# Scan tiles of two states by 64 channels, with the product by C on GpSimd

## The chip, the cores and the metric

The kernel runs on one core of one Trainium2 chip. A core has five engines that run their own instruction queues in order: TensorE (PE), VectorE (DVE), ScalarE (ACT), GpSimd (POOL) and SyncE (SP, which here only issues DMAs). The metric is the device time of one execution in microseconds; lower is better.

## The reference

The input x has the shape (8, 512, 48, 48): 8 samples, 512 channels, 2304 tokens. Two layers follow each other, each behind a group norm and with a residual sum. The first is causal linear attention with 8 heads. The second cuts the 512 channels into four blocks of 128 and runs a Mamba block on each in turn; each block's input is its own 128 channels plus the result of the block before. The part that the change touches is the recurrence inside a Mamba block, over 256 inner channels d and 16 states n:

```
delta = softplus(dt @ Wdt.T + bdt)                 # (tokens, 256)
dA  = exp(delta[d] * A[d, n]);  dBu = delta[d] * xs[d] * B[n]
h   = dA_t * h + dBu_t                             # for every token t
y_t = sum over n of h[d, n] * C_t[n]   + xs * D
out = (y * silu(z)) @ Wo.T
```

A[d, n] comes from a stored logarithm, B and C come from a projection of xs and differ for each token, not for each channel. All data are fp32.

## The kernel before

The 2304 tokens are cut into 6 chunks of `LC` = 384. For each sample, each of its four blocks (called scales in the code) and each chunk there are two functions.

`prepare` makes a chunk's inputs. PE multiplies the tokens with the convolution's taps (`xc`) and ACT makes `xs` (Silu); PE makes `z` and ACT the gate `sz`; PE makes the rows B, C and dt (`dbc`), ACT copies them out (`dbcs`), and SP writes B and C to scratch memory (`scr`). PE makes `v`, and the softplus of it is put together from Abs, Exp and Ln on ACT, one step on DVE (L332), two on POOL (L333, L334) and one on DVE (L335). DVE multiplies `dx` = delta * xs (L337). `prepare` of chunk c+1 stands in the program ahead of the scan of chunk c.

`scan` runs the recurrence. The partitions hold 128 channels, so there are two halves h; states are taken two at a time (`NG` = 2). For each pair, SP loads `bc` (L348): B and C of both states, 384 tokens each, sent to all 128 partitions, 768 KB; the pool holds two such tiles, and both halves use one. For each half ACT makes `dA` = exp(delta * A) for each state (L353), DVE makes `u` = B * dx for both (L357, 768 columns), DVE runs one `tensor_tensor_scan` for each state (L360, 384 columns), POOL copies the last column into `state` for the next chunk (L369), DVE multiplies by C (L370, 768 columns), and PE adds the products up over the states, as a matmul with the identity into the PSUM tile `yp` (L372). A last matmul with a diagonal matrix adds xs * D (L376). That makes 32 scans for a chunk. Then DVE multiplies `yp` by the gate (`yz`, L412), PE projects (`xm`, L415) and DVE takes the maximum (`fg`, L418). After the sixth chunk two means over all tokens give two sigmoids, and the next block starts from the result; nothing of the next block can start before.

The attention of the next sample is cut into 18 chunks of 128 tokens, which are spread over the last two blocks of the current sample. The attention of the first sample runs alone at the start. Its steps go through PE (`qk` L157, `v` L176, `kc` L186 and more), ACT (`ex` L168, `rl` L169) and DVE by turns; POOL makes its input `xn` (L148).

A scheduler orders the instructions of each engine's queue when the program is built, and puts in the waits. A queue runs in that order, so an instruction that waits holds everything behind it.

Of the kernel before, what the change touches and what calls it, by code (L numbers as in the profile page):

```python
# [9 lines left out]
F32 = mybir.dt.float32  # L10
# [7 lines left out]
T = 128  # tokens of an attention chunk  # L18
LC = 384  # tokens of a chunk of the state-space scan
NG = 2  # states that share one broadcast load and one product instruction  # L20
C_ID, C_MASK, C_GRP, C_ALL, C_TRI, C_SEL, C_BC = 0, 128, 256, 384, 512, 640, 672
C_END = C_BC + 512


def constants():
    """Matrices that the shapes alone give."""
    c = np.zeros((P, C_END), np.float32)
    p = np.arange(P)
    c[:, C_ID : C_ID + P] = p[:, None] == p[None, :]
    c[:, C_MASK : C_MASK + P] = p[:, None] <= p[None, :]  # L30
    c[:, C_GRP : C_GRP + P] = np.where(p[:, None] // 16 == p[None, :] // 16, 1.0 / 16.0, 0.0)
    same = p[:, None] % 64 == p[None, :] % 64
    c[:, C_ALL : C_ALL + P] = same
    c[:, C_TRI : C_TRI + P] = same & (p[:, None] // 64 <= p[None, :] // 64)
    for t in range(4):
        for half in range(2):
            head = 2 * t + half
            c[half * 64 : half * 64 + 64, C_SEL + t * 8 + head] = 1.0
            c[head, C_BC + t * P + half * 64 : C_BC + t * P + half * 64 + 64] = 1.0
    return c  # L40
# [3 lines left out]
def attention_then_mamba_kernel(  # L44
    ctx: ExitStack,
    tc: tile.TileContext,
    x: bass.AP,  # (B, 512, L)
    consts: bass.AP,
    wqkv: bass.AP,  # (512, 1536): input channel, output channel
    bqk: bass.AP,  # (128, 8)  # L50
    bv: bass.AP,  # (1, 512)
    win: bass.AP,  # (4, 128, 512): input channel, output channel
    wconv: bass.AP,  # (4, 1, 1024): tap, channel
    bconv: bass.AP,  # (4, 128, 2)
    wxp: bass.AP,  # (4, 128, 2, 40): columns B, C, dt
    wdt: bass.AP,  # (4, 8, 256)
    bdt: bass.AP,  # (4, 1, 256)
    alog: bass.AP,  # (4, 128, 2, 16)
    dskip: bass.AP,  # (4, 128, 2)
    wout: bass.AP,  # (4, 128, 2, 128)  # L60
    out: bass.AP,  # (B, 512, L)
# [15 lines left out]
    ps1 = ctx.enter_context(tc.tile_pool(name="ps1", bufs=4, space=PSUM))  # L77
    ps2 = ctx.enter_context(tc.tile_pool(name="ps2", bufs=1, space=PSUM))
# [10 lines left out]
    hbc = cst[0:8, C_BC : C_BC + 512].rearrange("p (t m) -> p t m", t=4)  # L89

# [13 lines left out]
    def group_norm(xt, name):  # L104
        """Scale and offset per channel, (128, 2), that normalise each 16 channels of xt."""
# [23 lines left out]
    def attention(b, X):  # L129
        """Puts x + attention(group norm of x) into X, a tile for each 128 channels; pauses  # L130
        after each chunk of tokens."""
# [11 lines left out]
        for i in range(L // T):  # L143
# [7 lines left out]
            # elu(t) + 1 = max(t, 0) + min(exp(t), 1)  # L151
# [30 lines left out]
            # The denominator: q . (sum of k over this head and those before it)  # L182
# [23 lines left out]
            # The numerator is linear in q, so q carries the denominator.  # L206
# [3 lines left out]
            for par in range(2):  # L210
                rows = slice(par * 64, par * 64 + 64)
                sc = one_bank(f"sc{par}_{n}").rearrange("p (o t) -> p o t", o=4)
                for o in range(4):
                    nc.tensor.matmul(sc[:, o, :], kT[rows, o, :], qT[rows, o, :], start=True, stop=True)
                m = apool.tile([P, 4, T], F32, tag=f"sm{par}", name=f"sm{par}_{n}")
                nc.vector.tensor_mul(m, sc, mask.unsqueeze(1).to_broadcast([P, 4, T]))
                sm.append(m)
# [15 lines left out]
            if i + 1 < L // T:  # L233
# [3 lines left out]
                kl = apool.tile([P, 4, P], F32, tag="kl", name=f"kl_{n}")  # L237
# [11 lines left out]
    def load_scale(b, s):  # L249
        """The weights of one of the four blocks."""  # L250
# [3 lines left out]
        # The convolution's taps scale the columns of the projection in front of it.  # L254
# [16 lines left out]
        dd = wpool.tile([P, 2, P], F32, tag="dd", name=f"dd_{n}")  # L271
        for h in range(2):
            nc.gpsimd.tensor_scalar_mul(dd[:, h, :], ident, pv[:, 2 + h : 3 + h])
        av = wpool.tile([P, 2, NS], F32, tag="av", name=f"av_{n}")
# [5 lines left out]
    def prepare(n, c, w, xi):  # L280
        """Projections of a chunk: its inputs to the scan, and the gate."""
        wi, wk, wo, wx, wd, pv, dd, av = w
        c0 = c * LC
        xc = ps2.tile([P, 2, 512], F32, tag="pp", name=f"xc_{n}_{c}")
        xs = mpool.tile([P, 2, LC], F32, tag="xs", name=f"xs_{n}_{c}")
        for h in range(2):
            for k in range(4):
                nc.tensor.matmul(  # L288
                    xc[:, h, 0:LC],
# [4 lines left out]
                )  # L294
        for h in range(2):
            nc.scalar.activation(xs[:, h, :], xc[:, h, 0:LC], AF.Silu, bias=pv[:, h : h + 1])
        zp = ps2.tile([P, 2, 512], F32, tag="pp", name=f"z_{n}_{c}")
        for h in range(2):
            nc.tensor.matmul(
                zp[:, h, 0:LC],  # L300
# [5 lines left out]
        sz = mpool.tile([P, 2, LC], F32, tag="sz", name=f"sz_{n}_{c}")  # L306
        nc.scalar.activation(sz, zp[:, :, 0:LC], AF.Silu)

        # B, C, dt, and a row of ones for dt's bias
# [9 lines left out]
        # softplus(v) = max(v, 0) + log1p(y), y = exp(-|v|);  # L319
        # log1p(y) = log(1 + y) + (y - ((1 + y) - 1)), the second term for the sum's rounding  # L320
        vp = ps2.tile([P, 2, 512], F32, tag="pp", name=f"v_{n}_{c}")
        for h in range(2):
            nc.tensor.matmul(
                vp[:, h, 0:LC], wd[32:41, h * P : (h + 1) * P], dbc[32:41, :], start=True, stop=True
            )
        y = mpool.tile([P, 2, LC], F32, tag="y", name=f"y_{n}_{c}", bufs=1)
        nc.scalar.activation(y, vp[:, :, 0:LC], AF.Abs)
        nc.scalar.activation(y, y, AF.Exp, scale=-1.0)
        delta = mpool.tile([P, 2, LC], F32, tag="delta", name=f"delta_{n}_{c}")
        nc.scalar.activation(delta, y, AF.Ln, bias=1.0)  # L330
# [3 lines left out]
        nc.gpsimd.tensor_tensor(delta, delta, y1, ALU.add)  # L334
        nc.vector.scalar_tensor_tensor(delta, vp[:, :, 0:LC], 0.0, delta, ALU.max, ALU.add)  # L335
        dx = mpool.tile([P, 2, LC], F32, tag="dx", name=f"dx_{n}_{c}", bufs=1)
        nc.vector.tensor_mul(dx, delta, xs)  # L337
        return xs, sz, scr, delta, dx

    def scan(n, c, w, pre, state):  # L340
        """The recurrence over a chunk, all states: D x + sum of C h."""
        wi, wk, wo, wx, wd, pv, dd, av = w
        xs, sz, scr, delta, dx = pre
        yp = psy.tile([P, 2, 512], F32, tag="yp", name=f"yp_{n}_{c}")
        src = scr.rearrange("(m n) l -> m n l", m=2)
        for g in range(0, NS, NG):
            bc = mpool.tile([P, 2, NG, LC], F32, tag="bc", name=f"bc_{n}_{c}_{g}")
            nc.sync.dma_start(out=bc, in_=src[:, g : g + NG, :].partition_broadcast(P))  # L348
            for h in range(2):
                m = f"{n}_{c}_{g}_{h}"  # L350
                dA = mpool.tile([P, NG, LC], F32, tag="dA", name=f"dA_{m}", bufs=3)
                for j in range(NG):
                    nc.scalar.activation(  # L353
                        dA[:, j, :], delta[:, h, :], AF.Exp, scale=av[:, h, g + j : g + j + 1]
                    )
                u = mpool.tile([P, NG, LC], F32, tag="u", name=f"u_{m}", bufs=3)
                nc.vector.tensor_mul(u, bc[:, 0], dx[:, h, :].unsqueeze(1).to_broadcast([P, NG, LC]))  # L357
                hs = mpool.tile([P, NG, LC], F32, tag="hs", name=f"hs_{m}")
                for j in range(NG):
                    nc.vector.tensor_tensor_scan(  # L360
                        hs[:, j, :],
                        dA[:, j, :],
                        u[:, j, :],
                        state[:, h, g + j : g + j + 1] if c else 0.0,
# [3 lines left out]
                if c + 1 < NC:  # L368
                    nc.gpsimd.tensor_copy(state[:, h, g : g + NG], hs[:, :, LC - 1])  # L369
                nc.vector.tensor_mul(u, hs, bc[:, 1])  # L370
                for j in range(NG):
                    nc.tensor.matmul(  # L372
                        yp[:, h, 0:LC], ident, u[:, j, :], start=(g + j == 0), stop=False
                    )
        for h in range(2):
            nc.tensor.matmul(yp[:, h, 0:LC], dd[:, h, :], xs[:, h, :], start=False, stop=True)  # L376
        return yp

    def mamba(b, X):
        """The four blocks in turn, from X to the output; pauses after each chunk of tokens."""  # L380
# [4 lines left out]
        for s in range(4):  # L385
# [4 lines left out]
            state = small.tile([P, 2, NS], F32, tag="state", name=f"state_{n}")  # L390
# [16 lines left out]
            for c in range(NC):  # L407
                cols, icols = slice(c * LC, (c + 1) * LC), slice(3 + c * LC, 3 + (c + 1) * LC)
                cur, pre = pre, (prepare(n, c + 1, w, xi) if c + 1 < NC else None)
                yp = scan(n, c, w, cur, state)  # L410
                yz = mpool.tile([P, 2, LC], F32, tag="tmp", name=f"yz_{n}_{c}", bufs=1)
                nc.vector.tensor_mul(yz, yp[:, :, 0:LC], cur[1])  # L412
# [16 lines left out]
            # sigmoids of the two means  # L429
# [15 lines left out]
    # The attention of a sample goes beside the last two blocks of the sample before it, which  # L445
    # leave the tensor engine free, and when two of that sample's four tiles are through.
# [74 lines left out]
```

## Time and profile before

| | |
|---|---|
| median of three runs | 16262.73 us (16234.96 to 16269.74) |
| span of the profiled execution | 16257.6 us |
| DVE busy | 13707.9 us (84%) |
| PE busy | 11687.1 us (72%) |
| ACT busy | 6667.4 us (41%) |
| POOL busy | 4851.7 us (30%) |
| chain that ended last | DVE 51%, PE 27%, issue 15% |

The profiled execution's own time is known as its span, from the first instruction to the last; the median of the runs is 5.1 us above it. The busy share is an average over stages: the attention alone at the start, the first two blocks of each sample (and all four of the last), where DVE has the scan and little else, and the last two blocks of the other samples, where attention shares the engines.

### The profile page before, as it was taken

To read this page: it belongs to the slowest core of one execution; us is meant where nothing else is said; L and a number is where in the kernel's file an instruction comes from. 1 tells how busy PE (TensorE), PEld (TensorE's weight loads), DVE (VectorE), ACT (ScalarE), POOL (GpSimd) and SP (SyncE) were. 2 spreads that over 40 slices of the span, in tenths; PEclk is the share of its full clock that TensorE was granted. 3 is DMA by queue.
4 is the path that set the end of the run, shared out by engine and by line. 5 is a ranking of instruction groups with operands and counts; after the bars stand their busy time and mean duration, and the time that the engine had idled before them with its cause. 6 is when DMAs were issued, how large, how long until landed. Compare 5 with 4: busy or idle time off the path is not lost.

```text
span 16257.6 us, 128122 instructions
## 1 busy us (share of the span) xinstructions
PE 11687.1 (72%) x42400; PEld 6603.9 (41%) x42400; DVE 13707.9 (84%) x16928; ACT 6667.4 (41%) x11513; POOL 4851.7 (30%) x4213
## 2 busy tenths in 40 slices
PE   8766876678766778667786677766777668776666
PEld 6533543235432355334452244533444234442322
DVE  2698888987899878998789987899777998789999
ACT  1344344443444434444334444344443444334444
POOL 0233232332333322332223322233322333223333
PEclk7788998889888889888998889988888888888888
DMA  0133222322233222332223322233222332223333
GB/s 31 49 98 89 72 75 85 99 86 71 77 89 98 85 71 74 92 97 82 71 73 96 98 77 74 69 100 100 76 72 72 100 95 78 66 73 95 96 96 93
DMA packets 470729, 1336.78 MB, mean 82 GB/s; under 512 B 49168, under 2 KB 59696, under 8 KB 461872
## 3 DMA queue, kind: packets, MB, share of 16 engines
q1 hardware_dynamic: 470064, 1328.60, 27.9%
q8 instruction: 334, 5.47, 0.1%
q14 instruction: 331, 2.71, 0.1%
HBM read 1281.28 MB, written 47.19 MB: 82 GB/s over the span
## 4 chain that ended last, share of the span: by engine, by line
DVE 51%; PE 27%; issue 15%; POOL 3%; ACT 3%; DMA 1%; DVEq 0%; SPq 0%; POOLq 0%; ACTq 0%
DVE hs L360 28%; DVE u L357 13%; PE qk L157 6%; DVE u L370 5%; PE yp L372 4%; PE v L176 3%; PE kc L186 2%; PE xm L415 2%; PE o L223 2%; PE xc L288 2%; PE o L220 1%; DVE dx L337 1%; POOL y L333 1%; POOL delta L334 1%; PE ds L241 1%
## 5 line engine op out<-in xcount | busy, mean ns | idle before, releaser
L372 PE MATMUL yp<-u,cst 128*128 128x384 f32 x12288 | 5693.4, 600 | 3126.1 <-DVE u L370 3123.6
L353 ACT ACTIVATE dA<-delta,av 128x384 f32<-128x384 f32 x6144 | 3453.9, 607 | 6896.7 <-DVE hs L360 6827.9
L360 DVE TENSOR_TENSOR_SCAN hs<-dA,state,u 128x384 f32<-128x384 f32 x5120 | 5204.2, 1053 | 25.8 <-ACT dA L353 1.0
L369 POOL COPY state<-hs 128x2 f32<-128x2 f32 x2560 | 3181.9, 1243 | 6692.4 <-DVE hs L360 6692.4
L372 PEld LDWEIGHTS yp<-u,cst 128*128 128x128 f32 x12288 | 2536.7, 225 | 5963.9 <-DVE u L370 4479.3
L357 DVE TENSOR_TENSOR u<-bc,dx 128x768 f32<-128x768 f32 x3072 | 2906.8, 961 | 69.8 <-PE yp L372 65.9
L370 DVE TENSOR_TENSOR u<-hs,bc 128x768 f32<-128x768 f32 x3072 | 2928.6, 953 | 22.6
L288 PE MATMUL xc<-xi,wk 128*128 128x384 f32 x3072 | 1385.8, 592 | 730.4 <-DVE delta L335 597.8
L288 PEld LDWEIGHTS xc<-xi,wk 128*128 128x128 f32 x3072 | 708.7, 237 | 1321.0 <-issue 635.1
L157 PEld LDWEIGHTS qk<-xn,wq_sb 128*128 128x128 f32 x9216 | 1075.8, 196 | 28.3 <-issue 14.0
L157 PE MATMUL qk<-xn,wq_sb 128*128 128x128 f32 x9216 | 1076.6, 279 | 0.0
L360 DVE TENSOR_TENSOR_SCAN hs<-dA,u 128x384 f32<-128x384 f32 x1024 | 974.3, 989 | 8.4
L171 DVE SCALAR_TENSOR_TENSOR f<-ex,rl 128x512 f32<-128x512 f32 x288 | 205.0, 712 | 761.2 <-ACT rl L169 761.2
L148 POOL TENSOR_SCALAR xn<-x,norm_a 128x128 f32<-128x128 f32 x576 | 271.1, 484 | 1719.1 <-PE v L176 1708.2
L353 ACT ACT_TABLE_LOAD x512 | 656.9, 1283 | 8.8
L415 PE MATMUL xm<-yz,wo 128*128 128x384 f32 x768 | 370.6, 615 | 351.9 <-DVE yz L412 351.9
L168 ACT ACTIVATE ex<-qk,bqk_sb 128x128 f32<-128x128 f32 x1152 | 435.8, 378 | 438.3 <-PE qk L157 398.7
L176 PE MATMUL v<-wq_sb,xn 128*128 128x512 f32 x1152 | 518.2, 592 | 0.0
L333 POOL TENSOR_TENSOR y<-y,y 128x768 f32<-128x768 f32 x192 | 416.6, 2170 | 234.2 <-DVE y L332 232.8
L169 ACT ACTIVATE rl<-qk,bqk_sb 128x128 f32<-128x128 f32 x1152 | 441.4, 383 | 0.0
L334 POOL TENSOR_TENSOR delta<-delta,y 128x768 f32<-128x768 f32 x192 | 417.5, 2174 | 15.1
L335 DVE SCALAR_TENSOR_TENSOR delta<-v,delta 128x768 f32<-128x768 f32 x192 | 182.4, 950 | 269.5 <-POOL delta L334 269.5
(98 smaller groups left out, 10133.1 us busy)
## 6 DMA issues: line engine op xcount, KB each, us to landing
bc<-scr SPq DMA_DIRECT2D x1536, 768.0 KB
x<-in_x SPq DMA_DIRECT2D x32, 1152.0 KB
out<-x SPq DMA_DIRECT2D x32, 1152.0 KB
wk<-in_wconv SPq DMA_DIRECT2D x32, 512.0 KB
scr<-dbcs SPq DMA_DIRECT2D x192, 48.0 KB
wi<-in_win SPq DMA_DIRECT2D x32, 256.0 KB
wo<-in_wout SPq DMA_DIRECT2D x32, 128.0 KB
wq_sb<-in_wqkv SPq DMA_DIRECT2D x4, 768.0 KB
```

What stands on the lines that cost most here:

```text
L157: nc.tensor.matmul(ps[:, o, :], wq_sb[:, kt, j * 512 + o * P : j * 512 + (o + 1) * P], xn[:, kt, :], start=(kt == 0), stop=(kt == 3),)
L176: nc.tensor.matmul(vps, xn[:, kt, :], wq_sb[:, kt, 1024:1536], start=(kt == 0), stop=(kt == 3))
L288: nc.tensor.matmul(xc[:, h, 0:LC], wk[:, k, h * P : (h + 1) * P], xi[:, c0 + k : c0 + k + LC], start=(k == 0), stop=(k == 3),)
L333: nc.gpsimd.tensor_tensor(y1, y, y1, ALU.subtract)
L334: nc.gpsimd.tensor_tensor(delta, delta, y1, ALU.add)
L353: nc.scalar.activation(dA[:, j, :], delta[:, h, :], AF.Exp, scale=av[:, h, g + j : g + j + 1])
L357: nc.vector.tensor_mul(u, bc[:, 0], dx[:, h, :].unsqueeze(1).to_broadcast([P, NG, LC]))
L360: nc.vector.tensor_tensor_scan(hs[:, j, :], dA[:, j, :], u[:, j, :], state[:, h, g + j : g + j + 1] if c else 0.0, ALU.mult, ALU.add,)
L369: nc.gpsimd.tensor_copy(state[:, h, g : g + NG], hs[:, :, LC - 1])
L370: nc.vector.tensor_mul(u, hs, bc[:, 1])
L372: nc.tensor.matmul(yp[:, h, 0:LC], ident, u[:, j, :], start=(g + j == 0), stop=False)
L415: nc.tensor.matmul(xm[:, 0:LC], wo[:, h, :], yz[:, h, :], start=(h == 0), stop=(h == 1))
```

## The change

The tile of the scan gets another layout. Its 128 partitions hold two states by 64 channels instead of one state by 128 channels. A half h of 128 channels is then two groups g of 64, and 16 states are 8 pairs. `NG` = 2 now counts pairs, so one group of work holds four scans of 384 columns: two pairs by two channel groups. There are 32 scans for a chunk, as before. Core of the diff:

```diff
-    ps1 = ctx.enter_context(tc.tile_pool(name="ps1", bufs=4, space=PSUM))
-    ps2 = ctx.enter_context(tc.tile_pool(name="ps2", bufs=1, space=PSUM))
+    ps1 = ctx.enter_context(tc.tile_pool(name="ps1", bufs=3, space=PSUM))
+    psa = ctx.enter_context(tc.tile_pool(name="psa", bufs=2, space=PSUM))
+    psx = ctx.enter_context(tc.tile_pool(name="psx", bufs=1, space=PSUM))
     psy = ctx.enter_context(tc.tile_pool(name="psy", bufs=1, space=PSUM))
...
-                m = apool.tile([P, 4, T], F32, tag=f"sm{par}", name=f"sm{par}_{n}")
+                m = apool.tile([P, 4, T], F32, tag=("rl", "ex")[par], name=f"sm{par}_{n}")
...
-                kl = apool.tile([P, 4, P], F32, tag="kl", name=f"kl_{n}")
+                kl = apool.tile([P, 4, P], F32, tag="xn", name=f"kl_{n}")
...
+            nc.scalar.activation(y[:, h, :], vp[:, 0:LC], AF.Abs)
+            nc.scalar.activation(r[:, h, :], vp[:, 0:LC], AF.Relu)
         nc.scalar.activation(y, y, AF.Exp, scale=-1.0)
...
         nc.vector.tensor_scalar(y1, y, 1.0, -1.0, ALU.add, ALU.add)
         nc.gpsimd.tensor_tensor(y1, y, y1, ALU.subtract)
-        nc.gpsimd.tensor_tensor(delta, delta, y1, ALU.add)
-        nc.vector.scalar_tensor_tensor(delta, vp[:, :, 0:LC], 0.0, delta, ALU.max, ALU.add)
-        nc.vector.tensor_mul(dx, delta, xs)
+        nc.gpsimd.tensor_tensor(r, r, y1, ALU.add)
+        nc.scalar.activation(y, y, AF.Ln, bias=1.0)
+        delta = y
+        nc.gpsimd.tensor_tensor(delta, delta, r, ALU.add)
+        dscr = dpool.tile([256, LC], F32, tag="dscr", name=f"dscr_{n}_{c}")
+        nc.sync.dma_start(out=dscr.rearrange("(h p) l -> p h l", h=2), in_=delta)
+        nc.gpsimd.tensor_tensor(dx, delta, xs, ALU.mult)
...
+    def scan(n, c, h, w, pre, state):
+        dr = mpool.tile([P, 2, LC], F32, tag="dr", name=f"dr_{n}_{c}_{h}")
+        dsrc = dscr.rearrange("(h g d) l -> h d g l", h=2, g=2)[h]
+        for i in range(2):
+            nc.sync.dma_start(out=dr[i * 64 : i * 64 + 64], in_=dsrc)
+        dxp = psx.tile([P, 2, 512], F32, tag="dxp", name=f"dxp_{n}_{c}_{h}")
+        for g in range(2):
+            nc.tensor.matmul(dxp[:, g, 0:LC], rep[:, g, :], dx[:, h, :], start=True, stop=True)
+        yp = psy.tile([P, 512], F32, tag="yp", name=f"yp_{n}_{c}_{h}")
+        nc.tensor.matmul(yp[:, 0:LC], dd[:, h, :], xs[:, h, :], start=True, stop=False)
+        for q in range(0, NS // 2, NG):
+            bc = mpool.tile([P, 2, NG, LC], F32, tag="bc", name=f"bc_{m}")
+            for i in range(2):
+                nc.sync.dma_start(out=bc[i * 64 : i * 64 + 64]..., in_=src[q // NG, i].partition_broadcast(64))
+            u = mpool.tile([P, NG, 2, LC], F32, tag="u", name=f"u_{m}", bufs=4)
+            nc.vector.tensor_mul(u, bc[:, 0]..., dxp[:, :, 0:LC]...)
+            for j in range(NG):
+                for g in range(2):
+                    dA = psa.tile([P, 512], F32, tag="dA", name=f"dA_{m}_{j}_{g}")
+                    nc.scalar.activation(dA[:, 0:LC], dr[:, g, :], AF.Exp, scale=...)
+                    nc.vector.tensor_tensor_scan(u[:, j, g, :], dA[:, 0:LC], u[:, j, g, :], ...)
+            if c + 1 < NC:
+                nc.scalar.copy(state[:, h, q : q + NG, :], u[:, :, :, LC - 1])
+            nc.gpsimd.tensor_tensor(u, u, bc[:, 1].unsqueeze(2).to_broadcast(shape), ALU.mult)
+            for j in range(NG):
+                for g in range(2):
+                    nc.tensor.matmul(yp[g * 64 : g * 64 + 64, 0:LC], pair_sum, u[:, j, g, :], start=False, ...)
...
+                for h in range(2):
+                    yp = scan(n, c, h, w, cur, state)
+                    nc.vector.tensor_mul(yz[:, h, :], yp[:, 0:LC], cur[1][:, h, :])
```

In words: delta is written to scratch memory (`dscr`) and read back in the new layout (`dr`); `dx` is copied into it by two matmuls with a 0/1 matrix into PSUM (`dxp`). `dA` goes to PSUM, one bank for each 384 columns, two banks in turn. The scan writes over `u`. A `bc` tile now serves one group of one half, and its two DMAs fetch four rows of 384 in one piece for each of 64 partitions. The state copy moves from POOL to ACT, the product by C from DVE to POOL, and the sum over states becomes a matmul with a 128 by 64 matrix (`pair_sum`) that also adds the two states of a pair. The softplus gets a Relu on ACT, and its last sum and `dx` move from DVE to POOL. `xc`, `z` and `v` now take single banks from the pool `ps1`, which has three banks instead of four and is shared with attention; two attention tiles take over the buffers of others (`sm` those of `rl` and `ex`, `kl` that of `xn`). The host reorders the columns of the projection weights and of A to match.

## The prediction

> **What bounds the kernel now.** I read the totals first, then the chain that ended last, then two stretches, then single rows.
>
> ```profile
> PE 11687.1 (72%) x42400; PEld 6603.9 (41%) x42400; DVE 13707.9 (84%) x16928; ACT 6667.4 (41%) x11513; POOL 4851.7 (30%) x4213
> ...
> DVE 51%; PE 27%; issue 15%; POOL 3%; ACT 3%; DMA 1%; DVEq 0%; SPq 0%; POOLq 0%; ACTq 0%
> ```
>
> DVE leads, but 84% is a mean over stages. The windows view, a plain stretch (scan alone) and one beside attention; columns PE, PEld, DVE, ACT, POOL busy, clock, DMA:
>
> ```profile
> 2700.00:2900.00 200.00, 127.87 (x300) 61.00 (x300) 197.23 (x212) 92.06 (x138) 83.00 (x64) 0.84 0.33 100
> 1800.00:2000.00 200.00, 159.00 (x739) 99.60 (x738) 166.77 (x212) 69.77 (x147) 48.18 (x46) 0.89 0.26 73
> ```
>
> Plain: DVE is busy 197 of 200 us and is the limit. Beside attention it is busy 167, PE 159: engines wait on each other in turn. By the starts of `yz` in the timeline a plain chunk takes 65 us (58 for the sixth, which prepares nothing), the step into the next block 38 more, so a plain block 5 x 65 + 58 + 38 = 421. A sample takes 1993 us, its two blocks beside attention (1993 - 842)/2 = 575.5 each, so each of their nine attention chunks adds 154.5/9 = 17.2. Attention alone ends at 597. Sum: 597 + 18 x 421 + 14 x 575.5 = 16232; 25.6 of the span 16257.6 are the tail, and the median is 5.1 above the span.
>
> The groups of the page (count | busy, mean ns of one | idle before, releaser):
>
> ```profile
> L372 PE MATMUL yp<-u,cst 128*128 128x384 f32 x12288 | 5693.4, 600 | 3126.1 <-DVE u L370 3123.6
> L353 ACT ACTIVATE dA<-delta,av 128x384 f32<-128x384 f32 x6144 | 3453.9, 607 | 6896.7 <-DVE hs L360 6827.9
> L360 DVE TENSOR_TENSOR_SCAN hs<-dA,state,u 128x384 f32<-128x384 f32 x5120 | 5204.2, 1053 | 25.8 <-ACT dA L353 1.0
> L369 POOL COPY state<-hs 128x2 f32<-128x2 f32 x2560 | 3181.9, 1243 | 6692.4 <-DVE hs L360 6692.4
> L357 DVE TENSOR_TENSOR u<-bc,dx 128x768 f32<-128x768 f32 x3072 | 2906.8, 961 | 69.8 <-PE yp L372 65.9
> L370 DVE TENSOR_TENSOR u<-hs,bc 128x768 f32<-128x768 f32 x3072 | 2928.6, 953 | 22.6
> ```
>
> DVE hardly ever waits for ACT (25.8 us): six `dA` of 384 columns are buffered. The others wait for DVE.
>
> **Removed from DVE.** L370 (2928.6), L335 (182.4) and L337 (181.6) go. `u` becomes 1536 instructions of 1536 columns; 768 columns with one operand in PSUM take 0.934 (`yz`, median), 512 take 0.676 (L216, mean), so 1.0 ns a column and 1.73 each: 2657 instead of 2907. Splitting `yz` costs 34. The scan with `dA` in PSUM has no row; `yz` and L357 (medians 0.934 and 0.935) show no price for PSUM, so I keep the busy time, 6178/6144 = 1.01 (ends 0.9 and 1.1). DVE loses 3.5 ms. Its work in a plain chunk is 32 x 1.01 + 8 x 1.73 + 2.4 (`yz`, L332, `fg`) = 48.5 us. If DVE stayed the limit, that would be the gain.
>
> **Added: the product on POOL.** From the views of single lines (min/median/max):
>
> ```profile
> L333 POOL TENSOR_TENSOR y<-y,y x192: 1795/2326/2532, 615.6 to 16129.5; 128x768 f32<-128x768 f32 x192
> ...
> L441 POOL TENSOR_TENSOR x<-x,fg x192: 982/1304/1443, 1015.4 to 16251.5; 128x384 f32<-128x384 f32 x192
> ```
>
> A line through the minima gives 0.98 + 3 x 0.813 = 3.42 us for 1536 columns, through the medians 1.30 + 3 x 1.02 = 4.37. In the timeline L333 takes 1.81 while DVE is idle (at 1038.9) and 2.38 while DVE scans (at 834.3). The new DVE instructions read only one tensor from SBUF and, as shown below, wait often, so I take 3.42 and keep 4.37 as the upper end. With four 768-column steps of 1.8 POOL has 8 x 3.42 + 7.2 + 0.4 = 35 us of work a chunk: no limit by amount.
>
> The Trainium skill, page "SBUF — State Buffer", section on who interferes with whom, says that a DVE instruction with two SBUF inputs contends with a GpSimd instruction that reads SBUF, and one with a single SBUF input does not. By that 3.42 holds and the sum below stands; without it 4.37 does, the third case below.
>
> **Added: a longer turn of `bc`.** This is what the DVE total hides. The two `bc` buffers now serve one group each, and a buffer is free only when POOL's product is done. Before, a `bc` DMA ended 4.8 us after its issue (median, from its packets: first packet at 1.0, then 256 of 3 KB), and the other tile covered 7.9 us. Now it has 128 packets of 6 KB; the 9 KB packets of `out` move 1180 KB in 3.0 us, so 786 KB take 2.0, plus 1.0 and the second issue (0.36, L348): 3.4 to 5.2, I take 3.6. One turn: DMA 3.6, issue 0.1, `u` 1.73, four scans 4.1, state copy on ACT 0.25 (an ACT instruction of 128x32 took 0.23) plus 0.1, product 3.42, other waits 0.3: 13.6 us for two groups, 54.4 a chunk. That is 6.8 a group against DVE's 5.8, so DVE idles 1.0 a group. Bytes for `dr` and `dscr` are 17% more, at a DMA share of 0.33: hidden. On SP, `dscr` waits for POOL's delta ahead of a `bc` whose product comes later on POOL anyway, and `scr` stands between the two halves of a `bc` that is not yet due: nothing. The state copies (8 x 0.25 a chunk) stand on ACT ahead of the next group's second `dA`, under `u`; uncovered they would cost 2 a chunk.
>
> **Added: waits across queues.** `dA` has two banks instead of six tiles, so whatever ACT waits for, DVE waits for two scans later. In the order in which the built program queues its instructions, repeated in the plain blocks, I find in chunks 2, 3 and 4 (a PE pass is 5693.4/12288 = 0.46; two passes a matmul):
> - PE has `v` of the next chunk behind three sums of group 0, which wait for POOL. ACT's Abs waits for `v`, and the third `dA` of the next group stands behind Abs, Relu and Exp. From the last scan: copy 0.35, product 3.42, six passes 2.8, `v` 0.9, four ACT steps of about 0.5, Exp 0.84, `dA` 0.61: 10.9. Cover is `u`, two scans and the idle 1.0, together 4.8. Lost 6.1.
> - `xc` stands behind the four sums of group 0 of the second half, and `xs`, a table load (1.28) and a `dA` behind it: 0.35 + 3.42 + 3.7 + 0.9 + 0.58 + 1.28 + 0.61 = 10.8, lost 6.0. In chunk 1 only half of `xc` is late: 3.
> - `yz` stands in DVE's queue after two scans of the next half and waits for the last product and its four sums: 7.5 against 4.8, plus its own 0.56: 3.3, twice a chunk.
> - Ln waits for POOL's L333 (in place), POOL's next sum for Ln, the next product behind both: 3.
>
> So chunks 2 to 4 take 54.4 + 6.1 + 6.0 + 6.5 + 3.0 = 76.0; chunk 1 66.9; chunk 0, where none of the first two waits stand, 63.9; chunk 5 60.9. Together 419.7. The step into the next block grows from 38 to 48: a third POOL sum instead of L335 (+0.9), `dscr` out and `dr` in, about 2.5 us each (5), product and split steps at the end (+4). A plain block takes 468 instead of 421.
>
> **Attention.** `kl` in the buffer of `xn` makes POOL's four L148 (0.48 each, with a start 2.4) wait for the chunk's last matmuls; alone at the start nothing covers that: 17 x 2.4 = 41, so 638. Beside the scan an attention chunk added 17.2. It could add only its DVE time, 7.6 (1098 us of its DVE rows by 144), filling DVE's waits; or its PE time, 24.1 (3469/144), laid into the chains above. I keep 17.2: 622.5 a block.
>
> **Sum.** 638 + 18 x 468 + 14 x 622.5 + 25.6 + 5.1 = 17808.
>
> PE's added passes (four `dxp` matmuls, 8 x 0.46 a chunk) are inside the waits. The same skill's "TensorEngine Tiling (Array Packing)", section on column tiling, says that matmuls onto 64 columns may run two at a time. L223, which has this form, took 335.0/2304 = 0.145 a pass against 0.121 for L186, so the trace shows no such gain; by the page the sums would halve and the total would be near 16800.
>
> **Rivals.** *Faster: the waits across queues are covered.* If ACT and PE run far enough ahead, only the turn remains: 6 x 54.4 + 48 = 374, with attention 528.5, total 638 + 6732 + 7399 + 31 = 14800. For it: PE and ACT have half their time free. Against: their queues are in order and the waits above stand in them. The sign changes where the mean plain chunk falls under 62.0 (32 x 6 x 62.0 + 32 x 48 + 14 x 154.5 + 669 = 16272); I have 70. *Much slower: POOL at 4.37 and attention at 24.1.* Turn and chains grow by 0.95 each: chunks 84, 84, 84, 73.9, 69.9, 66.9, step 49, block 512; with attention 729: 638 + 9216 + 10206 + 31 = 20090. For it: L333's median beside a busy DVE.
>
> **Numbers.** My case 0.62, own range 17000 to 19000; the faster rival 0.20; the slower one 0.15; about break-even 0.03. The runs spread by 0.2%, about what a measurement can tell from no change. Faster 0.21, same 0.02, slower 0.77. The range 15700 to 19500 leaves out the far halves of both rivals.
>
> **What would show it.** Right: DVE busy near 10.2 ms, idle before the scans with releaser ACT (over 1.5 ms), before `yz` with releaser PE, before `u` with releaser DMA; SP waiting for POOL; the product at 3.4. Wrong: product over 4, or plain stretches with DVE above 75% busy (48.5/62 is 78%), which would make it faster.

## The result, and the profile after

The changed kernel takes 17654.6 us (median of four runs, 17645.2 to 17662.1) against 16266.2 for the kernel before on the same chip: a ratio of 1.0854, 95% interval 1.0839 to 1.0869. The profiled execution has a span of 17655.0 us. The prediction was 17808. First the totals of the page:

```profile
PE 11077.4 (63%) x43936; PEld 5712.8 (32%) x43936; DVE 10582.7 (60%) x12128; ACT 7135.2 (40%) x13613; POOL 7402.1 (42%) x3573
...
POOL 3%; DVE 2%; DMA 2%; issue 2%; PE 1%; ACT 1%; SPq 0%; POOLq 0%; DVEq 0%; ACTq 0%
```

DVE lost 3125 us of busy time, and the span got 1397 us longer: DVE now waits 4.5 ms more. The chain of waits could be followed only for a tenth of the span (its shares add up to 11%), so the causes are read from stretches, groups and waits. The windows view, a plain stretch and one beside attention; columns PE, PEld, DVE, ACT, POOL busy, granted TensorE clock (1 is full speed), DMA share, GB/s:

```profile
2900.00:3100.00 200.00, 111.82 (x281) 39.08 (x281) 122.77 (x121) 91.46 (x156) 96.47 (x37) 0.66 0.41 102
2000.00:2200.00 200.00, 156.01 (x813) 99.14 (x812) 142.43 (x167) 78.88 (x176) 86.44 (x48) 0.85 0.33 78
```

In the plain stretch DVE is busy 123 of 200 us, where it was 197; no engine is above 62%. The waits view of DVE (us in total, times, longest), and the longest row of SP's:

```profile
DVE u L377 <- DMA bc<-scr: 2031.8, 697, 8.4
DVE yz L447 <- PE yp L404: 887.2, 283, 6.6
DVE u L391 <- ACT dA L385: 686.6, 357, 6.0
DVE y L340 <- ACT y L338: 656.0, 173, 18.3
DVE u L377 <- PE dxp L363: 533.6, 73, 13.9
```

```profile
SPq L371 <- POOL u L401: 9032.7, 1425, 23.4
```

DVE's largest is the load of `bc`; SP, which issues it, waits 9.0 ms in all for POOL's product. One turn of it can be read in the timeline of a plain chunk (start, duration, engine, line; in brackets the idle time before and its releaser):

```profile
2973.15 3.43 POOL L401 TENSOR_TENSOR u<-u,bc 128x1536 f32<-128x1536 f32 x1 [4.53 <-ACT state L400]
...
2976.61 8.41 SPq L371 DMA_DIRECT2D bc<-scr  x4
...
2982.44 1.75 DVE L377 TENSOR_TENSOR u<-bc,dxp 128x1536 f32<-128x1536 f32 x1 [2.32 <-DMA bc<-scr]
...
2984.30 3.74 DVE L391 TENSOR_TENSOR_SCAN u<-dA,state,u 128x384 f32<-128x384 f32 x4
...
2988.07 0.20 ACT L400 COPY state<-u 128x4 f32<-128x4 f32 x1 [0.32 <-DVE u L391]
2988.40 3.43 POOL L401 TENSOR_TENSOR u<-u,bc 128x1536 f32<-128x1536 f32 x1 [4.49 <-ACT state L400]
```

A product ends at 2976.58, SP issues the next load 0.03 us later (the row joins four issues), `u` starts 5.8 us after that, then come `u`, four scans, the state copy, and the next product on this buffer ends at 2991.83: 15.25 us for two groups. The groups of the page, as in the prediction (count | busy, mean ns | idle before, releaser):

```profile
L401 POOL TENSOR_TENSOR u<-u,bc 128x1536 f32<-128x1536 f32 x1536 | 5277.3, 3437 | 6915.1 <-ACT state L400 5374.2 <-DVE u L391 815.9 <-issue 363.7
L391 DVE TENSOR_TENSOR_SCAN u<-dA,state,u 128x384 f32<-128x384 f32 x5120 | 4875.6, 999 | 607.5 <-ACT dA L385 520.8 <-DVE u L377 1.4 <-ACT state L400 0.5
L404 PE MATMUL yp<-u,cst 128*64 128x384 f32 x12288 | 3669.9, 712 | 4890.6 <-POOL u L401 4887.8
L377 DVE TENSOR_TENSOR u<-bc,dxp 128x1536 f32<-128x1536 f32 x1536 | 2677.0, 1745 | 2683.3 <-DMA bc<-scr 2031.8 <-PE dxp L363 533.6 <-POOL u L401 84.4
```

Product, scan and `u` cost what the prediction took (3.44, 1.00 and 1.745 us). From the starts of the second `yz` of each chunk: in a plain block the first step, with the boundary, takes 116 us, then 75, 76, 75 to 78, 70 and 61.

### The profile page after: what moved, and what is told of

Same layout as the page of the kernel before. It is cut to its first block, busy times and chain, and to the rows that moved or that the text cites. A ratio compares the mean times of both kernels' runs of the same rounds, so it can differ in the third digit from the quotient of the medians.

```text
span 17655.0 us, 132567 instructions
## 1 busy us (share of the span) xinstructions
PE 11077.4 (63%) x43936; PEld 5712.8 (32%) x43936; DVE 10582.7 (60%) x12128; ACT 7135.2 (40%) x13613; POOL 7402.1 (42%) x3573
## 5 line engine op out<-in xcount | busy, mean ns | idle before, releaser
L401 POOL TENSOR_TENSOR u<-u,bc 128x1536 f32<-128x1536 f32 x1536 | 5277.3, 3437 | 6915.1 <-ACT state L400 5374.2
L404 PE MATMUL yp<-u,cst 128*64 128x384 f32 x12288 | 3669.9, 712 | 4890.6 <-POOL u L401 4887.8
L385 ACT ACTIVATE dA<-dr,av 128x384 f32<-128x384 f32 x6144 | 3552.2, 584 | 6361.2 <-DVE u L391 6278.6
L391 DVE TENSOR_TENSOR_SCAN u<-dA,state,u 128x384 f32<-128x384 f32 x5120 | 4875.6, 999 | 607.5 <-ACT dA L385 520.8
L377 DVE TENSOR_TENSOR u<-bc,dxp 128x1536 f32<-128x1536 f32 x1536 | 2677.0, 1745 | 2683.3 <-DMA bc<-scr 2031.8
L404 PEld LDWEIGHTS yp<-u,cst 128*64 128x64 f32 x12288 | 1030.8, 182 | 7005.0 <-POOL u L401 5937.3
L391 DVE TENSOR_TENSOR_SCAN u<-dA,u 128x384 f32<-128x384 f32 x1024 | 901.2, 936 | 181.6 <-ACT dA L385 165.8
L363 PE MATMUL dxp<-dx,cst 128*128 128x384 f32 x1536 | 843.8, 676 | 202.8 <-POOL dx L349 154.2
L180 DVE SCALAR_TENSOR_TENSOR f<-ex,rl 128x512 f32<-128x512 f32 x288 | 386.2, 1341 | 521.5 <-ACT rl L178 521.5
L365 PE MATMUL yp<-xs,dd 128*128 128x384 f32 x768 | 445.1, 670 | 385.6 <-DVE yz L447 385.6
L363 PEld LDWEIGHTS dxp<-dx,cst 128*128 128x128 f32 x1536 | 349.4, 258 | 728.1 <-issue 228.4
```

The lines of the kernel that those rows point to most:

```text
L180: nc.vector.scalar_tensor_tensor(f, ex, 1.0, rl, ALU.min, ALU.add)
L363: nc.tensor.matmul(dxp[:, g, 0:LC], rep[:, g, :], dx[:, h, :], start=True, stop=True)
L365: nc.tensor.matmul(yp[:, 0:LC], dd[:, h, :], xs[:, h, :], start=True, stop=False)
L377: nc.vector.tensor_mul(u, bc[:, 0].unsqueeze(2).to_broadcast(shape), dxp[:, :, 0:LC].unsqueeze(1).to_broadcast(shape),)
L385: nc.scalar.activation(dA[:, 0:LC], dr[:, g, :], AF.Exp, scale=av[:, 2 * h + g, q + j : q + j + 1],)
L391: nc.vector.tensor_tensor_scan(u[:, j, g, :], dA[:, 0:LC], u[:, j, g, :], state[:, h, q + j, g : g + 1] if c else 0.0, ALU.mult, ALU.add,)
```

## The experiments

The theory under test is the prediction's: a plain chunk is set by the turn of the two `bc` buffers through POOL's product, and by waits across in-order queues, where the sums on PE wait for POOL and ACT and DVE wait for what stands behind these sums. Rivals: POOL and DVE slow each other; PE's lower clock; ACT with only two `dA` banks. Runs without an interval are single times; each stands beside a run of the kernel before on the same chip, 16252 to 16275 us.

**Split tiles.** B and C in tiles of their own, the same bytes, so that B is free after `u`:

```diff
-            bc = mpool.tile([P, 2, NG, LC], F32, tag="bc", ...)
+            for k in range(2):
+                t = mpool.tile([P, NG, LC], F32, tag=("bb", "cc")[k], ...)
```

> B and C of a group in two tiles of 3 KB a partition instead of one of 6 KB, two buffers each, so that B is free after `u` and only C waits for the product on POOL. Theory (the two-buffer turn of `bc` through POOL's product is one of the two large causes): DVE's idle before `u` with releaser DMA, 2032 us in the changed kernel, falls under 500, DVE's busy time stays near 10.6 ms, and the time falls to 16000 to 16900. Rival (the waits across queues, where PE, ACT and POOL stand behind each other, set the chunk by themselves): the idle before `u` falls too, but comes back before the scans and `yz`, and the time stays at 17300 to 17700. Rival (DVE and POOL slow each other where they meet): more overlap makes the product longer than 3.6 us and DVE's busy time more than 10.9 ms.

15962 us, 1692 less than the changed kernel and 313 less than the kernel before. What DVE then waits for:

```profile
DVE u L380 <- PE dxp L363: 969.9, 245, 13.5
DVE yz L450 <- PE yp L407: 776.6, 305, 6.5
...
DVE u L380 <- DMA bb<-scr: 420.6, 141, 4.9
DVE y L340 <- ACT y L338: 412.9, 102, 15.2
DVE u L394 <- ACT dA L388: 387.9, 251, 3.3
```

The wait for the load fell from 2032 to 421 us; plain chunks take about 60 instead of 75. One tile that held what is read early and what is read late cost more than the whole loss of 1388 us against the kernel before. The wait for `dxp` nearly doubled (534 to 970), so part of the queue waits had been hidden under the turn.

**Product on DVE.** One word of the changed kernel:

```diff
-            nc.gpsimd.tensor_tensor(u, u, bc[:, 1]..., ALU.mult)
+            nc.vector.tensor_tensor(u, u, bc[:, 1]..., ALU.mult)
```

> The product by C back on DVE, all else as in the changed kernel; POOL keeps only the steps of `prepare` and the block's end. DVE gets 1536 instructions of 1536 columns, by the old product's 953 ns for 768 some 1.9 us each, 2.9 ms in all. Theory (POOL's 3.4 us stand in every chain that DVE waits for): DVE is then the limit, its work in a plain chunk is 48.5 + 15.3 = 64, the chunk takes 64 to 67 instead of 75, and the time falls to 16200 to 16900 although DVE has 2.9 ms more to do. Rival (the lower clock of PE, or ACT with two dA banks, sets the chunk): the 15 us a chunk come on top in part, 17700 to 19500.

16785 us: 870 less, although DVE is busy 2440 us more (13022). The product on DVE:

```profile
L401 DVE TENSOR_TENSOR u<-u,bc 128x1536 f32<-128x1536 f32 x1536 | 2845.4, 1852 | 261.2 <-ACT state L400 256.0
```

So taking POOL out of the chain is worth more than POOL's help; the rival (PE's clock or ACT set the chunk) would have made it longer. That POOL and DVE slow each other is a small part of it here: the attention step `f`, which reads two SBUF tensors, is 0.19 ms shorter in all. But a plain chunk takes 71, not 64 to 67, and DVE was busy only 154 to 175 us of 200: some waits across queues stay.

**Without prepare.**

```diff
-                cur, pre = pre, (prepare(n, c + 1, w, xi) if c + 1 < NC else None)
+                cur, pre = pre, pre
```

> `prepare` of chunks 1 to 5 of every block is left out, and these chunks scan the inputs of chunk 0 again (so convolution, gate, B, C and delta are made once a block). Theory, as the prediction had it: without prepare's instructions in the queues only the turn of `bc` and `yz` remain, every chunk takes what the sixth takes now, 61 us instead of 75, so a plain block 6 x 61 + 48 to 50 = 415 instead of 474, and the time falls by about 32 x 60 = 1900, to 15500 to 16000. Rival (the waits come from the turn and from contention, and prepare only fills them): chunks stay over 68 and the time over 16800.

15832 us, 1822 less. Chunks take 63 us, all alike, where 61 was expected, and a plain block 422 on the mean instead of 475. The 53 us are what `prepare` costs a block. DVE's own work in it is one instruction of 0.56 a chunk at the median, and over the whole kernel DVE's busy time fell by only 197 of the 1822 us, so nearly all of it is DVE waiting for the others; this run does not part their work from the order in which it stands in their queues. The prediction's sum had 419.7 - 6 x 60.9 = 54. No run has this change and the split tiles together, so whether the two gains add up is not shown.

**Sums onto 128 columns.**

```diff
-                        yp[g * 64 : g * 64 + 64, 0:LC],
-                        pair_sum,
+                        yp[:, 0:LC],
+                        k_all,
```

> The sum over states as a matmul onto all 128 columns: the same count of matmuls and moving columns, but each adds both channel groups onto both halves of `yp`, so the two groups are not kept apart. Theory (matmuls onto the two halves of the columns overlap in the changed kernel: 844 ns a matmul at the median, but 8 passes in 2.8 us or less): one pass goes from 0.30 back to about 0.46, the sums of a group from 2.4 to 3.7 us, and since they stand in the chains to `yz`, `v` and `xc` a chunk grows by 3 to 5 us: 18200 to 18700. Rival (no overlap, the shorter times are gaps in the records; or the sums are covered): 17550 to 17800.

17984 us, 329 more, between the two. The row of the sum here, then the eight passes of one group here and in the changed kernel (start, duration):

```profile
L404 PE MATMUL yp<-u,cst 128*128 128x384 f32 x12288 | 5848.5, 630 | 4062.0 <-POOL u L401 4060.4
```

```profile
2990.22 5.49 PE L404 MATMUL yp<-u,cst 128*128 128x384 f32 x8 [6.65 <-POOL u L401]
```

```profile
2983.97 2.83 PE L404 MATMUL yp<-u,cst 128*64 128x384 f32 x8 [4.50 <-POOL u L401]
```

5848.5/12288 = 0.476 us a pass against 3669.9/12288 = 0.299: onto 64 columns the passes of the two groups do overlap; in the trace nearly every second one starts 6 to 7 ns after the one before it, and none does here. But the granted clock in the plain stretch is 0.79 here and 0.66 in the changed kernel, with the same instructions but for this matmul, and part of what the overlap gains on PE is given back in other matmuls: `dxp`, the same in both, takes 512 ns on the mean here and 676 there. In both kernels PE is idle before the sums for 4.1 to 4.9 ms, until POOL's product is done. Where the 329 us lie says more: a plain block takes 478 us instead of 475, one beside attention 623 instead of 603, so in the plain blocks, which the theory was about, the shorter sums are worth next to nothing.

**`dA` in SBUF, four buffers** (and for the room `u` with three instead of four).

```diff
-                    dA = psa.tile([P, 512], F32, tag="dA", ...)
+                    dA = mpool.tile([P, LC], F32, tag="dA", ..., bufs=4)
```

> The changed kernel with `dA` in SBUF, four buffers instead of two PSUM banks; for the room `u` has three buffers instead of four. Theory (what ACT waits for reaches DVE two scans later; four would cover more of it): DVE's idle before the scans with releaser ACT, 687 us, falls under 300, the time by 300 to 600, to 17050 to 17400. Rival (what the scan reads matters: a scan with `dA` and `u` both in SBUF meets POOL's product, which reads SBUF too): the scan goes from 1.00 to 1.2 us or more, the product from 3.44 to 4, the time over 18000. Second rival (neither: the chains behind POOL decide): 17500 to 17800.

18005 us, 351 more. The wait for ACT is gone, as the theory had it (687 to under 70 us), but the scan got longer. Durations of the scan (min/median/max), here and in the changed kernel:

```profile
L390 DVE TENSOR_TENSOR_SCAN u<-dA,state,u x5120: 904/993/4261, 763.2 to 17978.5; 128x384 f32<-128x384 f32 x197
```

```profile
L391 DVE TENSOR_TENSOR_SCAN u<-dA,state,u x5120: 904/993/1019, 760.0 to 17629.9; 128x384 f32<-128x384 f32 x197
```

The median is the same; with both operands in SBUF some scans take up to 4.26 us, about a scan plus a product of 3.4. The mean is 1.21, and DVE's busy time rises by 1305 us. The product hardly changes (3.49). With `dA` in PSUM no scan took longer than 1.02. What two banks alone cost stays open: the wait went and the longer scans came in the same run, and `u` lost a buffer.

**`kl` in its own buffer.**

```diff
-                kl = apool.tile([P, 4, P], F32, tag="xn", ...)
+                kl = apool.tile([P, 4, P], F32, tag="kl", ...)
```

> The changed kernel with a buffer of its own for the attention tile `kl` again; for the room the weights `wo` and `wd` have one buffer instead of two. Theory, by the prediction's step: the four `xn` of POOL no longer wait for the last matmuls of the attention chunk before; attention alone gets 41 us shorter or more (its end is 71 us later than in the kernel before), and beside the scan a chunk gains 0 to 2.4: 17350 to 17610. Rival (the 71 us come from the three banks instead of four, or from the shared `sm` tiles): within 20 us of 17655.

17558 us, 97 less. The first `dA` starts at 637.2 instead of 691.3 (620.4 before): 54 of the 71 us that the start had lost come from this wait. That is all that the attention itself lost: its last step `x` ends at 591.7 in the kernel before, 644.0 in the changed one and 590.7 here. The rest of the 71 lies between that step and the first `dA`, 28.6 us before and 47.3 after, so in the first `prepare`, where delta now goes out and comes back through memory.

**Old layout, product on POOL.** The missing corner of a table, the kernel before with

```diff
-                nc.vector.tensor_mul(u, hs, bc[:, 1])
+                nc.gpsimd.tensor_tensor(u, hs, bc[:, 1], ALU.mult)
```

> The kernel before with one edit: its product by C (768 columns, both operands in SBUF) goes from DVE to POOL; layout, buffers and the rest stay. With the kernel before, the changed kernel and the changed kernel with the product on DVE this makes a table of two layouts by two engines. Theory (a product on POOL lengthens the chain from the scan to the buffers and the sum; what matters is how many buffers stand against it, and the old layout has two `bc` tiles that serve both halves, three `u` and two `hs`): DVE's busy time falls to about 11 to 12 ms, but a plain chunk falls less, since POOL has 16 x (1.8 + 1.0) = 45 us a chunk of products and state copies: 15200 to 16300. Rival (DVE's scans and `u` read two tensors in SBUF here and meet POOL's product: scans of 1.2 us, products of 2.3): 16300 to 17800.

18456 us, outside of both ranges. The theory's 11 to 12 ms of DVE time was wrong; the rival named the mechanism, but its range was too low. Its groups:

```profile
L360 DVE TENSOR_TENSOR_SCAN hs<-dA,state,u 128x384 f32<-128x384 f32 x5120 | 6526.9, 1318 | 144.9 <-POOL state L369 2.4 <-POOL u L370 1.7 <-DVE u L357 1.5
L370 POOL TENSOR_TENSOR u<-hs,bc 128x768 f32<-128x768 f32 x3072 | 6388.7, 2080 | 1292.6 <-DVE hs L360 1196.1 <-PE yp L372 68.7 <-issue 12.7
...
L357 DVE TENSOR_TENSOR u<-bc,dx 128x768 f32<-128x768 f32 x3072 | 4249.5, 1395 | 902.2 <-PE yp L372 590.2 <-DMA bc<-scr 260.5 <-POOL u L370 47.5
```

and the durations of `u` (min/median/max):

```profile
L357 DVE TENSOR_TENSOR u<-bc,dx x3072: 919/958/2635, 621.8 to 18423.9; 128x768 f32<-128x768 f32 x192
```

2.93 ms of products left DVE, and its busy time rose, from 13708 to 14276 us. Here `u` and the scan read two tensors from SBUF. At the median they cost what they did (0.96 and 1.00); the longest `u` takes 2.64, about itself (0.96) plus a product on POOL (1.80). The table, in us: old layout, product on DVE 16266; old, POOL 18456; new, DVE 16785; new, POOL 17655; new, POOL and split tiles 15962. A product on POOL costs 2190 us in the old layout and 870 in the new one. In the old one the scans and `u` that stay on DVE grew by 3.0 ms, adding up their durations; in the new one, with an operand of each in PSUM, their longest are 1.02 and 1.76 us. That the operands make the whole difference is not shown: the layouts differ in their buffers too, and `dA` in SBUF cost the new one only 351. Nor was the split kernel run with its product on DVE, so the table does not say on which engine the product is best once the tiles are split.

The Trainium skill, page "SBUF — State Buffer", section on who interferes with whom, states this: a DVE instruction with two SBUF inputs and a GpSimd (POOL) instruction that reads SBUF exclude each other for a whole instruction, and one with a single SBUF input is free of it outside of what the page calls 2-port perf modes. The rows of scan and `u` agree (longest scan 1.02 with one SBUF operand, 4.26 with two; longest `u` 2.64). The prediction had left out the page's condition on the modes; `y1`, in the last section, shows that a single SBUF input alone is not enough.

**Another order.** The split kernel, with some instructions held behind others on their engine's queue (no wait added). The core, shortened and with comments put in:

```diff
+    def behind(ins, prev):
+        tc.add_manual_dep(ins.ins, prev.ins.name, NoSync)
...
+        for q0, u0 in pend:                     # sums of the third and fourth group
+            sums(q0, u0, nh[2] if nh else None) # behind dxp of the next half
...
+            if q == 0:
+                late(sc)                        # yz of the half before, behind the first group's scans
```

> The kernel with split tiles for B and C, with the same instructions in another order of the queues. The matmuls `dxp` of the next half stand ahead of the sums of the third and fourth group; `yz` stands behind the four scans of the next half's first group instead of two; in the blocks without attention beside, `xc` of the next prepare stands behind the sums of the second group of the second half, `xs` behind the last `dA` of the chunk, and the first sums of a chunk behind `v`. Theory (what is left of the waits after the split is a matter of order in the queues: 970 us before `u` for `dxp`, 777 for `yz`, 413 and 388 for ACT): half to all of 2500 us goes, plain chunks take 50 to 54 instead of 60, the time is 13900 to 14900. Rival (the order only moves the waits on, or POOL with 35 us of products a chunk and ACT's steps follow each other too closely): 15400 to 16200.

15095 us, 867 less than the split kernel with the same work: less gain than the theory's range, more than the rival's. Plain chunks take 58, not 50 to 54. The waits here:

```profile
DVE y L352 <- ACT y L350: 808.5, 120, 15.5
DVE u L415 <- PE dxp L373: 638.1, 145, 11.0
DVE u L429 <- ACT dA L423: 604.2, 339, 5.1
...
DVE yz L496 <- PE yp L391: 400.2, 172, 6.5
...
DVE u L415 <- DMA bb<-scr: 100.1, 109, 2.3
```

The wait for `dxp` fell from 970 to 638, the one for `yz` from 777 to 400; the one of `y1` for ACT rose from 413 to 809. Scans wait longer for ACT, too (388 to 604), so that the four waits named in the theory fell from 2548 to only 2451 in all: they moved from one place to another, and the rival is right on these. The gain lies beside them: the load of B (421 to 100), `f` for ACT (643 to 376) and `x` for PE (609 to 412). `f` and `x` are steps of attention, and the block times say the same: a plain block went from 400 to 383 us, one beside attention from 579 to 539. So 18 plain blocks gave some 300 us and the 14 others some 560, although the holds on `xc`, `xs` and the first sums stand in the plain blocks alone. The holds on `dxp` and `yz`, which stand in all blocks, are those that paid there; which of the two did is not shown.

**Steps at the ends of groups.** Further such holds, and

```diff
-        nc.vector.tensor_scalar(y1, y, 1.0, -1.0, ALU.add, ALU.add)
+        nc.gpsimd.tensor_scalar(y1, y, 1.0, -1.0, ALU.add, ALU.add)
```

> The reordered kernel with three more steps: the step `y1` = (y + 1) - 1 goes from DVE to POOL; `kl` has its own buffer again (and `wo`, `wd` one each); and in the plain blocks the steps of `prepare` are placed one group earlier and at the ends of groups, each behind the last `dA` of a group and ahead of the first of the next (`xs`, copy, Abs to Exp, `sz`, Ln), POOL's steps one behind each product, `xc` ahead of the second group's sums. Theory (58 us of a plain chunk against 48.5 us of DVE work are what is left of waits: `y1` for ACT 808 us, `dxp` 638, scans for `dA` 604, `yz` 400): plain chunks take 50 to 53, the time is 14100 to 14500. Rival (POOL, with 27.5 us of products and 8.6 of prepare's steps, now sets the chunk through `u` and `yz`): 56 to 58 a chunk, 14700 to 15000.

15052 us, 43 less: outside of both ranges. `kl`, too, has its own buffer here, and the first `dA` starts 41 us earlier for it, so holds and moved step together came to about nothing. Plain chunks take 53 to 56, which gained 6 us a block; the blocks beside attention got 8 us longer; and the moved step costs on POOL five times what it does on DVE at the median (0.56):

```profile
L369 POOL TENSOR_SCALAR y<-y x192: 2766/2775/2797, 616.6 to 14934.1; 128x768 f32<-128x768 f32 x192
```

**All together.** That step back on DVE, `z` in its old place beside attention:

> The kernel with the steps of `prepare` at the ends of groups, with `y1` back on DVE (behind the second group's last scan in the plain blocks) and `z` in its old place in the blocks with attention. Theory (the 2.78 us of the step on POOL took back what the order had brought, and `z` behind Exp delayed `yz` beside attention): plain chunks 52 to 55, the blocks with attention as in the reordered kernel or a little less, 14700 to 14950. Rival (POOL's other steps and the loads of B are what is left): 14950 to 15100.

14851 us (four runs, 14845 to 14873) against 16273 for the kernel before (seven runs): a ratio of 0.9128, interval 0.9113 to 0.9143, in the theory's range. Plain chunks take 54 to 56 between the first and the sixth, a plain block 371 on the mean (424.6 before, 475 in the changed kernel), one beside attention 541, no less than in the reordered kernel. DVE's idle time fell from 7072 us in the changed kernel to 4483, its work hardly (10583 to 10368). A plain stretch:

```profile
2900.00:3100.00 200.00, 123.10 (x372) 45.91 (x372) 162.35 (x161) 111.00 (x198) 128.30 (x48) 0.78 0.51 137
```

DVE is still busy only 162 of 200 us, so this is not its limit either.

## Why the prediction was right, step by step

Sign, size and mechanism held: 17808 forecast, 17655 measured, 0.9% less. The terms, some of which were off and made up for each other, which is luck:

- *DVE's work*: 3.5 ms fewer forecast, 3.1 measured (10.58 instead of 10.2 ms busy). Scan and `u` were right. Instructions with two SBUF tensors grew behind POOL's products: `f` from 712 ns (L171 before) to 1341 on the mean, and 681 in the run with the product on DVE. That is 0.18 of the 0.38 ms; the rest was not followed. The prediction had named the rule and looked at the new instructions only, not at those that stayed. The rows of `f` in the changed kernel and with the product on DVE:

```profile
L180 DVE SCALAR_TENSOR_TENSOR f<-ex,rl 128x512 f32<-128x512 f32 x288 | 386.2, 1341 | 521.5 <-ACT rl L178 521.5
```

```profile
L180 DVE SCALAR_TENSOR_TENSOR f<-ex,rl 128x512 f32<-128x512 f32 x288 | 196.2, 681 | 264.8 <-ACT rl L178 262.9
```

- *The product*: 3.42 forecast, 3.44 measured; the upper end of 4.37 was not reached. L333's slow median, from which that end came, arose beside DVE instructions with two SBUF operands, most of which the change took away: the same form in the changed kernel (L342) takes 1.80 to 1.82. In the run with the old layout and the product on POOL the product has a mean of 2.08 with a minimum of 1.80.
- *The turn of `bc`*: 13.6 forecast for two groups, 15.25 in the timeline. The scans took 3.74 instead of 4.1. The DMA was the term that was too small: 3.6 was worked out from packets of 9 KB of another transfer, while the two halves of `bc` land 5.0 us after their issue (median; 4.8 for the old tile of the same 768 KB, from which I had gone down). Four turns of 15.25 are 61.0, which is what the sixth chunk takes: the forecast of 60.9 for it came right by luck, since its 6.5 for the waits before `yz` made up for a turn that was 1.65 too short, four times.
- *Waits across queues*: the total was right (53 us a block for `prepare` by the run without it, 54 in the sum), the places less so. Chunk 1 takes 75 instead of 66.9, chunk 4 takes 70 instead of 76. DVE's idle before scans is 0.69 ms, where over 1.5 was forecast; the chain through `v` shows up as `y1` waiting for ACT (0.66 ms), because this DVE instruction stands in the queue ahead of the scans that would wait.
- *A PE pass*: 0.46 forecast, 0.30 measured. The prediction weighed the skill's "TensorEngine Tiling (Array Packing)", section on column tiling, against L223 and kept the trace's side. The page was right on the pass: the run with 128 columns takes 0.476. The reading of L223 was at fault: in the trace of the kernel before, 902 of its 2304 passes start 6 to 7 ns after the one before, so they overlap too, and the mean of 0.145 a pass hid it. The total by the page, 16800, was still wrong, since undoing the overlap costs 329 us and not 1000, nearly all of it beside attention.
- *Attention*: alone it loses 52 us where 41 were forecast, and the wait priced accounts for all of it (53 in the run with `kl` in its own buffer). A block beside attention takes 603 on the mean instead of 622.5, so that an attention chunk adds (603 - 475)/9 = 14.2 and not 17.2: a step toward the lower end of 7.6, where attention fills DVE's idle time. What filled it was not traced.
- *The sum*: a plain block takes 475 on the mean instead of 468. Against the forecast that is +11 for attention alone, +2 for the first block (470 us from the end of attention), 17 x 7 = +119, 14 x -19.4 = -272, and -14 for the end (17 us behind the last block where 30.7 were added): together -154, the whole difference. Plain blocks that were too cheap and attention that was too dear nearly cancel.

The faster rival failed on its own condition: the waits were not covered, and the mean plain chunk stayed over 62.0. Its DMA term of 3.6 was too small as well. The split kernel shows how near it was: with chunks of 60 it is 2% faster than before.

## What to carry to other kernels

When work moves to another engine, list every buffer that the moved instruction frees and ask how long it is now held; if one tile holds data for an early and a late reader, split it. Then look at who reads what: in these runs POOL's products never lengthened a scan or a `u` with one SBUF operand, and blocked those with two for up to a whole product, so an operand in PSUM can be worth more than a deeper buffer (here 351 us, with one buffer of `u` less). Where no engine is busy for more than two thirds of a stretch, as here, look at how long buffers are held and at the order in the queues: splitting one tile took off 1692 us, and holding a few instructions behind others 867 more, neither changing any work.

## What was not expected of the hardware

- A blocked DVE instruction takes up to its own time plus that of a whole POOL product: 2.64 where the two add up to 0.96 + 1.80, 4.26 where they add up to 0.99 + 3.49. It happens to a DVE instruction with a single SBUF tensor, too. `y1` with its 768 columns in 0.56 us runs faster than the 0.94 of two-tensor instructions of that size, and its longest is 3.2 us longer than its median:

```profile
L340 DVE TENSOR_SCALAR y<-y x192: 533/560/3773, 673.3 to 17516.9; 128x768 f32<-128x768 f32 x192
```

- On POOL an instruction with one tensor and two constants (2.78 us for 768 columns) takes longer than one with two tensors (1.80).
- The granted clock is lower with the shorter sums, 0.66 against 0.79 in the plain stretch, in two kernels that differ only in these matmuls. The Trainium skill's "TensorE: Matmul & The Clock Gate", part 1, says that the clock follows how busy the array has lately been; the rows agree with that (PE busy 125 and 112 us of 200), but no run here varies the idle time alone. The row of the run onto 128 columns, to be read beside that of the plain stretch above:

```profile
2900.00:3100.00 200.00, 124.79 (x285) 62.13 (x286) 122.69 (x121) 92.31 (x157) 94.46 (x35) 0.79 0.41 99
```
